# Inverting layer 3's last four half rows on ScalarE, and moving the safety flag behind the last residual

## The chip, the cores and the metric

The kernel runs on one core of one Trainium2 chip. The metric is the device time of one execution in microseconds. Three executions of the kernel before took 3706.58, 3706.09 and 3710.97 us; the median is 3706.58. One further execution was profiled. Its trace is what all rows below are from, with times counted from the start of its span.

The engines are named as in the profile: PE is TensorE's matmul, PEld its weight load, DVE is VectorE, ACT ScalarE, POOL GpSimd and SP SyncE, which here only issues DMA transfers. A `q` behind a name (SPq, DVEq) is the engine's instruction queue.

## The reference, cut to what matters

The input is four images of 56 x 56 pixels with 256 channels. Each of four layers adds to it a branch that starts with a group norm. Layer 0 is a 7x7 neighbourhood attention, layer 1 a dense graph step over chunks of 1024 tokens, layer 2 a neighbourhood attention in two dilations. The change lies in layer 3, a shifted-window attention with 8 heads of 32 channels on windows of 7 x 7 pixels:

```python
xs = jnp.roll(x, (-3, -3), axis=(1, 2))             # x: group norm of the stream
qkv = windows(xs) @ qkv_weight.T + qkv_bias         # q is scaled by 32 ** -0.5
attn = einsum('whnd,whmd->whnm', q, k) + bias + mask
attn = softmax(attn, axis=-1)
out = einsum('whnm,whmd->wnhd', attn, v) @ proj_weight.T + proj_bias
x = x + jnp.roll(windows_back(out), (3, 3), axis=(1, 2))
```

## The kernel before

`direct_blocks` does the four layers without a row maximum in its softmaxes: it takes Exp of the logits as they are, multiplies by the values, and divides by the sums. That holds only while no sum becomes too large, so all along the way sums and inverses are added into four small watch tiles. At the end `unsafe` (L2444 on) tests the sums of these tiles against a limit, and a matmul with a column of ones counts the good partitions into `flag`. Every engine reads the flag (`values_load`, L2533) and branches (L2534): where it is set, only the memset of L2535 runs; where it isn't, a second, careful implementation computes everything anew. A block with a branch hint (L2529) surrounds the test.

Layer 3 works on 32 rows of windows: row r is one of eight window rows of one of four images, with 8 windows of 49 pixels, 392 columns. A row has two halves of four heads (hq = 0, 1). Below, (30,1) is the second half of row 30. A half row goes through these steps, each of them one or two instructions per engine:

- logits (L1024): matmuls into two pairs of PSUM banks, tags `s0` and `s1`, one buffer each;
- ScalarE takes Exp of `s1` with its sum (L1028), GpSimd multiplies it with an exponentiated mask (L1029); VectorE adds the mask to `s0` (L1031), ScalarE takes its Exp (L1032);
- products (L1040): the sums over the keys, by a matmul with ones, and the products with the values, into the two banks of tag `o`, or for (30,1) and (31,1) into two buffers of tag `m`;
- finish: VectorE inverts the sums (L2295), GpSimd adds the inverse to a watch tile (L997, `seen`), and VectorE multiplies products and inverse (L2297).

The output projection of a row (`project_out`, L952) follows two rows later: matmuls into a bank, ScalarE adds the bias (L2317), GpSimd adds the residual (L2319), SyncE stores the row (L2176). Its second step also issues that store. `last_row` does row 31 by itself: it adds the bias to the residual ahead (L2333), splits the projection by the two halves of the attention (L2337), and VectorE adds straight from PSUM (L2344).

`attend_quads` runs the half rows as a pipeline: logits of one, fill work, products of the one before. In layer 3 the order on TensorE, VectorE, ScalarE and GpSimd is the order in which the code issues; SyncE's order, and all of layer 0, are left to a scheduler. After the loop the last half rows, (31,0) and (31,1), are written out by hand, with the projections of rows 29, 30 and 31 between them. The projections of row 29's second half and row 30's first half share the two banks of `s1`, and row 30's second half takes `s0`.

## Time and profile before

| what | value |
|---|---|
| median of three executions | 3706.58 us (3706.09 to 3710.97) |
| profiled execution | 3706.61 us |
| its span, first to last instruction | 3704.8 us |
| granted TensorE clock | 0.997 |
| TensorE busy, matmuls | 3646.7 us, 98% |
| VectorE, ScalarE, GpSimd busy | 59%, 40%, 49% |
| window 3680 to 3698: TensorE, VectorE, ScalarE, GpSimd busy | 13.71, 16.16, 6.63, 12.77 of 18.00 us |
| window 3698 to 3704.8: VectorE busy, all others | 0.21 us, 0 |

In a timeline row the first number is the start, the second the length from the first start to the last end of the merged instructions; then come engine, line of the kernel, operation, output and inputs, shapes and how many. In brackets stands the idle time of the engine just before and what ended it. In the chain view a row is a stretch of the path that ended last, and "issue" is time in which nothing that the profile shows was waited for.

### The profile page before, as it was taken

The numbers are of one execution on the slowest core, as the hardware profiler recorded it, in microseconds if no ns is written. First come the engines' busy times: TensorE is split into PE (matmuls) and PEld (weight loads), VectorE is DVE, ScalarE is ACT, GpSimd is POOL, SyncE is SP. The second block draws the span as 40 slices with busy tenths as digits, with TensorE's granted clock in tenths as the row PEclk, the third lists the DMA queues.
The fourth block names the chain that finished last, engine by engine and source line by source line (L and its number), as shares of the span: only waits on it lengthen the run. The fifth ranks groups of instructions, "written<-read, shape, count | busy, mean of one in ns | idle before, by whom it ended". The sixth has DMA issues, their size and how long they took to land.

```text
span 3704.8 us, 112520 instructions
## 1 busy us (share of the span) xinstructions
PE 3646.7 (98%) x48954; PEld 2480.4 (67%) x48954; DVE 2197.9 (59%) x4177; ACT 1479.3 (40%) x3137; POOL 1803.7 (49%) x1952
## 2 busy tenths in 40 slices
PE   8999999999999999999999999999999999999998
PEld 4666666677776777767777777776666666555554
DVE  5787777544445444554444643445777777677776
ACT  5666665422222222222222222223666666444444
POOL 4777877421234222352222521124877777555555
PEclk9999999999999999999999999999999999999999
DMA  7554444200011000101001000002454444544443
GB/s 232 163 168 138 145 126 135 110 7 24 24 30 38 13 19 20 29 28 23 20 19 24 27 15 11 11 21 72 120 146 144 136 131 125 166 133 134 133 134 103
DMA packets 278151, 304.95 MB, mean 82 GB/s; under 512 B 33638, under 2 KB 268778, under 8 KB 277294
## 3 DMA queue, kind: packets, MB, share of 16 engines
q1 hardware_dynamic: 275408, 296.03, 26.5%
q8 instruction: 386, 6.32, 0.7%
q10 hardware_dynamic: 672, 1.48, 0.1%
q0 software_dynamic: 1568, 0.16, 0.1%
q14 instruction: 117, 0.96, 0.1%
HBM read 205.04 MB, written 92.55 MB: 80 GB/s over the span
## 4 chain that ended last, share of the span: by engine, by line
PE 90%; DVE 5%; DMA 1%; ACT 1%; POOL 1%; issue 1%; SPq 0%; DVEq 0%; ACTq 0%; POOLq 0%
PE ps_m L952 19%; PE ps_o L1698 14%; PE ps_s L1576 14%; PE ps_v L1703 13%; PE ps_m L981 6%; PE ps_o L1113 6%; PE ps_s L1080 6%; PE ps_t L1684 3%; PE ps_o L1040 2%; PE ps_s L1024 1%; PE ps_m L1541 1%; DVE st L896 1%; DVE rs L1286 1%; DVE e L1087 1%; PE ps_m L1769 1%
## 5 line engine op out<-in xcount | busy, mean ns | idle before, releaser
L1608 DVE TENSOR_TENSOR acc<-acc,ps_v 128x257 f32<-128x257 f32 x1088 | 457.7, 422 | 774.5 <-PE ps_v L1703 751.6
L1703 PE MATMUL ps_v<-xw,e 128*128 128x257 f32 x2208 | 611.0, 381 | 3.4 <-DVE xnT L1553 2.2
L1698 PE MATMUL ps_o<-xw,at 128*128 128x257 f32 x2208 | 609.0, 379 | 0.0
L1576 PE MATMUL ps_s<-xnT,xd 128*128 128x512 f32 (+3 forms) x1344 | 571.4, 548 | 3.9 <-DVE xnT L1553 3.9
L1687 ACT COPY at<-ps_t 128x512 f32<-128x512 f32 (+3 forms) x332 | 170.7, 514 | 953.8 <-PE ps_t L1684 953.5
L1703 PEld LDWEIGHTS ps_v<-xw,e 128*128 128x128 f32 x2208 | 413.4, 189 | 144.6 <-issue 83.2
L1102 POOL TENSOR_TENSOR b<-e 124x448 f32<-124x448 f32 (+5 forms) x498 | 484.8, 995 | 7.2 <-ACT e L1088 0.3
L1698 PEld LDWEIGHTS ps_o<-xw,at 128*128 128x128 f32 x2208 | 419.1, 190 | 60.1
L952 PE MATMUL ps_m<-xn,w_wqkv 128*32 128x392 f32 x4096 | 374.3, 494 | 1.2 <-ACT xn L942 0.9
L1569 POOL TENSOR_SCALAR xd<-xnT,vec 128x128 f32<-128x128 f32 x192 | 116.3, 615 | 476.2 <-PE ps_s L1576 476.0
L1579 ACT ACTIVATE e<-ps_s 128x512 f32<-128x512 f32 x336 | 185.4, 552 | 353.0 <-PE ps_s L1576 349.7
L1576 PEld LDWEIGHTS ps_s<-xnT,xd 128*128 128x128 f32 x1344 | 225.4, 191 | 141.3 <-issue 126.2
L1091 POOL TENSOR_TENSOR e<-e,bias 119x784 f32<-119x784 f32 (+5 forms) x128 | 241.5, 1887 | 151.3 <-ACT e L1090 150.5
L1091 POOL TENSOR_TENSOR e<-e,m0t 126x672 f32<-126x672 f32 (+3 forms) x128 | 238.6, 1864 | 154.7 <-ACT e L1090 147.9
L1113 PEld LDWEIGHTS ps_o<-e,vp 124*32 124x32 f32 (+5 forms) x8000 | 193.8, 110 | 96.4 <-issue 81.5
L1002 ACT ACTIVATE no<-rs 128x168 f32<-128x168 f32 (+2 forms) x256 | 93.9, 367 | 387.7 <-DVE rs L2028 176.8
L952 PEld LDWEIGHTS ps_m<-xn,w_wqkv 128*32 128x32 f32 x4096 | 124.1, 109 | 175.7 <-issue 127.5
L2028 DVE RECIPROCAL rs<-ps_o 128x196 f32<-128x196 f32 (+2 forms) x128 | 175.7, 1373 | 101.7 <-PE ps_o L1113 82.8
L1088 ACT ACTIVATE e<-e 126x672 f32<-126x672 f32 (+5 forms) x256 | 219.6, 858 | 16.3 <-DVE e L1087 4.2
L1113 PE MATMUL ps_o<-e,vp 124*32 124x112 f32 (+5 forms) x8000 | 220.7, 248 | 0.3 <-DMA vp<-vd 0.2
L1090 ACT ACTIVATE e<-ps_s 126x672 f32<-126x672 f32 (+5 forms) x256 | 206.3, 806 | 5.4 <-PE ps_s L1080 5.4
L981 PE MATMUL ps_m<-w_wqkv,xn 128*32 128x256 f32 x3136 | 198.0, 382 | 1.8 <-DVE v L987 1.6
(240 smaller groups left out, 5985.8 us busy)
## 6 DMA issues: line engine op xcount, KB each, us to landing
x<-xr SPq DMA_DIRECT2D x64, 392.0 KB
x<-in_x SPq DMA_DIRECT2D x53, 448.0 KB
x<-x SPq DMA_DIRECT2D x60, 392.0 KB
xr<-x SPq DMA_DIRECT2D x60, 392.0 KB
vd<-v SPq DMA_DIRECT2D x72, 256.0 KB
xr<-in_x SPq DMA_DIRECT2D x32, 392.0 KB
xr<-x SPq DMA_DIRECT2D x28, 448.0 KB
x<-xr SPq DMA_DIRECT2D x28, 448.0 KB
```

Of the source, the lines that this page charges most:

```text
L952: nc.tensor.matmul(pm[j * HD:(j + 1) * HD, :n], lhsT=w[:, h, col + j * HD:col + (j + 1) * HD], rhs=rhs(h), start=(h == 0), stop=(h == CC - 1))
L981: nc.tensor.matmul(pm[i:i + HD, j * C:(j + 1) * C], lhsT=xn[:, h, first + i:first + i + HD], rhs=w[:, h, :], start=(h == 0), stop=(h == CC ...
L1080: nc.tensor.matmul(s[j // 2][:nk, j % 2, (2 * i + u) * nq:(2 * i + u + 1) * nq], lhsT=k(j, u), rhs=q(j), start=True, stop=True)
L1088: newest.append(nc.scalar.activation(ev, ev, AF.Exp))
L1090: nc.scalar.activation(ev, sv, AF.Exp)
L1091: nc.gpsimd.tensor_tensor(parts(ev), parts(ev), w["emask"], ALU.mult)
L1102: nc.gpsimd.tensor_tensor(w["b"][a][:nk, :, :2 * nq].rearrange("p h (i c) -> p h i c", i=2), ev[:, :, :, 0, :], ev[:, :, :, 1, :], ALU.add)
L1113: nc.tensor.matmul(w["o"](k, i)[j * HD:(j + 1) * HD], lhsT=ones[:nk, :HD] if k else v(j, u), rhs=w["b"][j // 2][:nk, j % 2, i * nq:(i + 1) ...
L1576: nc.tensor.matmul(s[:, :n], lhsT=xd[j][:, h, :], rhs=xnT[:, h, first * P:last * P], start=(h == 0), stop=(h == CC - 1))
L1608: nc.vector.tensor_tensor(acc[:, i, :], acc[:, i, :], pv[:, :C + 1], ALU.add)
L1698: nc.tensor.matmul(out[j][:, :C + 1], lhsT=e[:, col(i)] if i == j else at[:, col(i)], rhs=xw[:, i, :], start=(i == j), stop=(i == NB - 1))
L1703: nc.tensor.matmul(pv[:, :C + 1], lhsT=e[:, col(i)], rhs=xw[:, j, :], start=True, stop=True)
```

## The change

Six edits, all but one at the end of the kernel.

- The sums of (30,0), (30,1), (31,0) and (31,1) are no longer inverted by VectorE. ScalarE takes Ln of them and then Exp of the negative, which is the inverse; the second one also sums into a new watch tile `late` in place of GpSimd's `seen`. The Exp of L1032 of these four half rows sums into `late` too. The inversions are issued at places of their own.
- A table load for the set of activation functions that holds Exp and Ln is put at the start of `direct_blocks`; before, one was placed ahead of the first activation.
- Row 30's first half projects into `s0` and its second half into `s1`; row 31's second output tile takes `s0`.
- The watch tiles are summed earlier, apart from `late` and one other. The comparison goes to GpSimd and gives each of five columns 1/128 where it is good and less than zero where it isn't. A matmul behind the last projection adds the partitions up, and one reduction on VectorE, behind the last residual, takes the smallest of the five as the flag.
- The block with the branch hint is gone.
- The second tile of row 31's store is issued by ScalarE, the first by SyncE as before.

In the instruction order of the changed program three things shift that the diff does not name: the table load stands ahead of the loads of `vec` and `group` on ScalarE; in layer 0 two of SyncE's loads and one of VectorE's additions change places with their neighbours; at the start of layer 3 SyncE's load of the x tile of row 3 stands behind the loads of two masks, `w_wp` and `v`.

```diff
+    tables = [s.name for s in act_sets.SETS].index("natural_log_exp_and_others")
+    nc.scalar.add_instruction(mybir.InstLoadActFuncSet(..., act_func_set_id=tables, ins=[], outs=[]))
...
-            nc.scalar.activation(ev[0], ev[0], AF.Exp)
+            nc.scalar.activation(ev[0], ev[0], AF.Exp, accum_out=w.get("sum0"))
...
+            def invert():
+                rs = box["rs"] = pool.tile([P, WC], FP, tag="rs", name="rs3")
+                nc.scalar.activation(rs, box[1][:, :WC], AF.Ln)
+                nc.scalar.activation(rs, rs, AF.Exp, scale=-1.0, accum_out=late[:, i + 4:i + 5])
+
             def finish():
-                rs = pool.tile([P, WC], FP, tag="rs", name="rs3")
-                nc.vector.reciprocal(rs, box[1][:, :WC])
-                seen(rs)
+                rs = box.get("rs")
+                if rs is None:
+                    rs = pool.tile([P, WC], FP, tag="rs", name="rs3")
+                    nc.vector.reciprocal(rs, box[1][:, :WC])
+                    seen(rs)
...
-                for m, tag in enumerate(("o", "s1")):
+                for m, tag in enumerate(("o", "s0")):
...
-                    transfer(4, r, x, 1, slice(m, m + 1))
+                    transfer(4, r, x, 1, slice(m, m + 1), (nc.sync, nc.scalar)[m])
...
+        late = pool.tile([P, 8], FP, name="late", bufs=1)
+        nc.vector.memset(late, 0.0)
...
+        before[0]["invert"]()
         u3, u4 = quad(r, 0), quad(r, 1, single=True)
         out = project_out(r - 2)
         logits(u3, lambda: (out[0](), done()))
         products(held)
+        held["invert"]()
         logits(u4, held["done"])
         products(u3)
-        pair = psum_tile("s1", 1, 2)
-        out[1](pair[:, 0])
+        for i in (0, 1, 3):
+            bounds.add_up(i)
+        out[1](psum_tile("s1", 1, 2)[:, 0])
+        u3["invert"]()
+        u3["done"]()
         out = project_out(r - 1)
         first, second = last_row(r)
-        out[0](pair[:, 1])
-        u3["done"]()
+        out[0](psum_tile("s0", 1, 2)[:, 0])
         products(u4)
-        out[1](psum_tile("s0", 1, 2)[:, 0])
+        u4["invert"]()
+        out[1](psum_tile("s1", 1, 2)[:, 0])
         u4["done"]()
-        for i in (1, 3, 2):
-            add_up_watch(i)
+        bounds.add_up(4, late)
+        bounds.add_up(2)
+        bounds.compare()
         first()
         second()
+        bounds.count(ps_m(), ones[:, :1])
...
-def unsafe(tc, t, n, flag):
-    nc.vector.tensor_tensor(t[:, :n], t[:, :n], t[:, :n], ALU.mult)
-    nc.vector.tensor_scalar(t[:, :n], t[:, :n], SUM_MAX ** 2, None, ALU.is_le)
-    nc.vector.tensor_reduce(t[:, n:n + 1], t[:, :n], AX.X, ALU.min)
-        nc.tensor.matmul(ok, lhsT=t[:, n:n + 1], rhs=t[:, n + 1:], start=True, stop=True)
-        nc.vector.tensor_scalar(flag, ok, P - 0.5, None, ALU.is_ge)
+    def compare(self):
+        t = self.sums
+        self.nc.gpsimd.tensor_tensor(t, t, t, ALU.mult)
+        self.nc.gpsimd.tensor_scalar(t, t, SUM_MAX ** 2, 1.0 / P - 1.0, ALU.is_le, ALU.add)
+
+    def count(self, ps, one):
+        ok = ps[:1, :5]
+        self.nc.tensor.matmul(ok, lhsT=one, rhs=self.sums, start=True, stop=True)
+        self.nc.vector.tensor_reduce(self.flag, ok, AX.X, ALU.min)
...
-                with tc.block():
-                    tc.mark_branch_hint_location("safe", hint="LikelyTaken", engines=list(mybir.ALL_ENGINES))
-                    add_up_watch(0)
-                    unsafe(tc, bounds, n, flag)
```

## The prediction

> **What bounds the kernel now.** First the page's head, its table of busy times and its chain. TensorE is busy 98% of the span, and the chain that ended last is 90% TensorE.
>
> ```profile
> span 3704.8 us, 112520 instructions
> PE 3646.7 (98%) x48954; PEld 2480.4 (67%) x48954; DVE 2197.9 (59%) x4177; ACT 1479.3 (40%) x3137; POOL 1803.7 (49%) x1952
> PE 90%; DVE 5%; DMA 1%; ACT 1%; POOL 1%; issue 1%; SPq 0%; DVEq 0%; ACTq 0%; POOLq 0%
> ```
>
> So an edit that does not take matmuls away can only gain where TensorE is not the one that ends last. The edits lie in the last 27 us. There I read the timeline of each engine from 3678.7 us on. VectorE first:
>
> ```profile
> 3678.93 2.61 DVE L2295 RECIPROCAL rs<-ps_o 128x392 f32<-128x392 f32 x1 [1.75 <-PE ps_o L1040]
> ...
> 3682.96 2.60 DVE L2295 RECIPROCAL rs<-ps_m 128x392 f32<-128x392 f32 x1
> ...
> 3686.15 0.97 DVE L1031 TENSOR_TENSOR e<-ps_s,m3b 98x784 f32<-98x784 f32 x1
> 3687.03 2.60 DVE L2295 RECIPROCAL rs<-ps_o 128x392 f32<-128x392 f32 x1
> ...
> 3690.88 2.61 DVE L2295 RECIPROCAL rs<-ps_m 128x392 f32<-128x392 f32 x1 [0.64 <-PE ps_m L1040]
> ...
> 3695.89 0.69 DVE L2344 TENSOR_TENSOR xr<-xr,ps_s 128x343 f32<-128x343 f32 x3
> 3696.49 0.56 DVE L2526 TENSOR_REDUCE bounds<-watch 128x1 f32<-128x392 f32 x1
> ...
> 3698.01 0.15 DVE L2453 TENSOR_SCALAR flag<-n_safe 1x1 int32<-1x1 f32 x1 [0.37 <-PE n_safe L2452]
> 3703.13 0.06 DVE L2535 MEMSET flag<- 1x1 int32 x1 [4.97 <-issue]
> ```
>
> VectorE works almost without a gap: four reciprocals of 2.6 us, and behind the last residual (3696.58) another 1.58 us of bound checks up to the flag (3698.16). Then TensorE and ScalarE, which wait meanwhile:
>
> ```profile
> 3685.37 1.50 PE L952 MATMUL ps_s<-attn,w_wp 128*32 128x392 f32 x16
> 3688.54 1.52 PE L952 MATMUL ps_s<-attn,w_wp 128*32 128x392 f32 x16 [1.67 <-ACT pr L2317]
> ```
> ```profile
> 3684.92 0.19 ACT L1028 ACTIVATION_READ_ACCUMULATOR e<-ps_s 98x1 f32 x1
> 3687.16 0.86 ACT L1032 ACTIVATE e<-e 98x784 f32<-98x784 f32 x1 [2.04 <-DVE e L1031]
> 3687.92 0.57 ACT L2317 ACTIVATE pr<-ps_s,vec 128x392 f32<-128x392 f32 x1
> ```
>
> TensorE stands idle 1.67 us because L2317 of the projection sits on ScalarE behind the Exp of L1032, which waits for L1031 on VectorE, which stands behind a reciprocal. Last, the chain at the very end: after the flag has been read, 3.93 us in which nothing runs but the branch.
>
> ```profile
> 3698.20 0.54 DVEq L2533
> ...
> 3698.90 3.93 issue
> ```
>
> **Reciprocals to ScalarE.** Removed: 4 x 2.6 us of L2295 on VectorE and 4 x 1.03 us of L997 on GpSimd. Added: on ScalarE four Ln and four Exp of 128x392, each taken as 0.57 us (L2317, same shape, from PSUM), and eight accumulator reads of 0.19 (L1028). No row shows an Ln. Lower bound 0.52 (0.86 of L1032 less half its elements at about 0.33), upper bound 0.86 (a whole L1032); I take 0.57, the same shape. A pair with its read is 0.57 + 0.05 + 0.57 + 0.11 = 1.3 us, against 2.65 for the reciprocal.
>
> I follow the new order, engine by engine, with a half row as (row, half). (30,0): its sums are ready at 3678.8; Ln and Exp take ScalarE to 3680.2, so L2297 ends at 3680.8 (before 3682.15), and L1031 of (31,0) at 3681.8 (before 3683.04). The L1028 behind the pair slips from 3679.83 to 3680.2. Its next waiter, L1029, has 1.8 us of idle time before it. L1032 of (31,0), now with an accumulator, runs 3681.87 to 3682.8. Ln and Exp of (30,1) follow to 3684.1; L2297 to 3684.7, L1031 of (31,1) to 3685.7 (before 3687.12). What is queued behind this pair is L1028 of (31,1), whose logits TensorE has by 3683.65: it starts at 3684.12, as early as before (3684.20), because the pair stands where the wait stood.
>
> TensorE then takes L952 of row 29 when that L1028 frees the bank, 3685.10 (before 3685.37). Row 30's first half goes to the other bank (the tags are swapped), free at 3685.7, so it starts 1.32 us later, at 3686.42, in place of 3688.54. From there TensorE never waits in my sum: products of (31,1) from 3687.76 (1.34 later; L1029 is done at 3687.0), row 30's second half 3689.14 (1.38), first halves of row 31 at 3690.46 and 3691.12 (1.32, 0.66), the second half at 3691.78 (0.66). Before it was 3694.22: 2.44 us won. ScalarE must keep up: L1032 of (31,1) to 3686.7, L2317 to 3687.3, pair to 3688.5, L2317 to 3689.1, pair to 3690.4, L2317 (waits for TensorE) to 3691.3, two L2333 to 3692.4. L2297 of (31,1) ends at 3691.0, 0.75 us before TensorE wants it. L2344 comes 0.99 us after the second half's start, as before: 3692.77, with the second tile to 3694.14.
>
> **Flag.** The check over 392 columns, L2447 and L2448 leave the end: the sums move ahead, where VectorE now waits, and two small operations go to GpSimd behind its last L2319 (3692.7) and end at 3693.2 (0.20 and 0.22 each by L925 and L926). The count on TensorE stands behind its last matmul and waits for GpSimd: 3693.5. Left behind the residual is one reduction of 0.16 (L2449): flag at 3694.33, before 3698.16. That is 3.83 us, all of it on the end's chain. If GpSimd were late, its cover is the 0.6 us from 3693.5 to the residual's end.
>
> **Two queues.** On SyncE the last two transfers' issue (0.81 us) goes to ScalarE. SyncE's first pair ends at 3694.4 and delays its flag read by 0.07. ScalarE issues from 3694.2 to 3695.05 and branches 0.8 us after the others; SyncE meets it only at the closing barrier, whose waits take SyncE over 1 us after the branch: nothing. The writes themselves run under the 3.9 us of the branch, as before.
>
> **Branch.** The block with a prefetch hint and its two jumps go. In the DMA view no instruction transfer lies between 3692.6 and 3698.0, where the hints stand, and the instruction queues run only from 3699.7 on, after the branch. So the hint fetched nothing; I take 0. Bounds: 0.5 us less, if the fetch no longer follows so close behind the output's writes, and another fetch round, 3.9 us more.
>
> **Table load.** It moves ahead of two DMA issues on ScalarE. The trace shows one load of 1.28 us, and `vec` landing at 3.83 (L853 starts on it). `vec` lands up to 1.28 us later, at 5.1. VectorE uses it now between the two first statistics (4.58 to 5.13), and the next tile lands at 5.97: covered. SyncE's seventh load waits for the first tile (4.53) instead of `vec` (3.93), with six tiles of 1.2 us ahead of it: covered. Layer 0's other shifted loads are used microseconds later. I take +0.1, bounds -0.5 and +1. The changed program has one table load on this path, and the trace no switch to price. The Trainium skill (ScalarE: Activation LUTs, section What ACT_TABLE_LOAD costs) states an estimated price for what speaks against this edit: 2.66 us for each switch of the set of functions. By it, eight switches between Ln and Exp would add 21 us, and the sum would be 3724. The same page lists one set that holds both, the one loaded here, and by that the sum stays.
>
> **Layer 3's opening.** A 0.06 us memset shifts SyncE's order: the x load (392 KB) goes behind two mask loads, w_wp and v. TensorE waits 0.6 us for v at 3220.15 (list of waits); v comes about 1 us sooner. The x tile then lands near 3220, its 1.66 us of L945 end just before VectorE's next job (3222.02). Gain between 0 and 0.6; I take 0.3.
>
> **Sum.** 3.76 + 0.3 - 0.1 = 4.0 us. The profiled execution took 3706.61 (span 3704.8 and 1.8 around it), beside a median of 3706.58. Forecast 3702.6 us. A measurement of this kernel tells about 0.2% (7.4 us) from no change; this is 0.11%.
>
> **Rivals.** (a) The branch costs one more fetch round without its hint: 3702.6 + 3.85 = 3706.4. For it: 3.93 us even with the hint, so the code is not at hand. Against it: no transfer by the hint. (b) Slower: the sequencers, unhinted, run on into the fallback's code and fetch two rounds before the target's. Place: after the flag read; price 7.7 us; 3710.3. It decides from 4.0 us on. (c) ScalarE becomes the bound: Ln and Exp cost 0.86 each. The pairs of (30,0) and (30,1) lie on the path to 3685.10 and add 1.2 us; the last two add 1.2, less the 0.75 of slack: 0.4. Then 3702.6 + 1.6 = 3704.2. For it: my ScalarE row is full from 3686.7 to 3690.4. (d) More is won: layer 0 and layer 3's opening give their 0.5 and 0.6, and the fetch is quicker by 3 us beside idle queues: 3699 or less. Nothing in the profile speaks for the last. (e) The new flag reads false and the fallback runs: thousands of us more; the five sums of 128 times 1/128 are exact, so 1%.
>
> **How the numbers follow.** Forecast 0.60, (a) 0.13, (b) 0.07, (c) 0.13, (d) 0.06, (e) 0.01. The forecast's own bounds: layer 0's -0.6 and +0.9, layer 3's opening -0.3 and +0.3, the branch -0.5, a shorter Ln and Exp -0.2, the two close runs' 0.5 either way: 3700.5 to 3704.3. Range 3700.5 to 3707.0: above it takes in (a) with the same 0.5. Forecast, (a) and (c) hold 0.86, some 0.8 with runs like the third (3710.97). Faster by over 0.2% (below 3699.2): (d) and a little of the spread, 0.08. Slower (above 3714.0): half of (b), and (e), 0.04. Within: 0.88.
>
> **What would show it.** No reciprocal of L2295's kind after the one at 3673.98; TensorE without a gap over 0.3 us from the second-half projection of row 29 to the end; flag about 0.2 us after the last residual; some 3.9 us from flag read to the closing memset. A gap on TensorE that ends on ScalarE's Ln or Exp shows (c); 7 us or more after the flag shows (a) or (b). Wrong would be a shift before 3670 us of more than 1 us.

## The result, and the profile after

| | median | runs | lowest to highest |
|---|---|---|---|
| before | 3708.55 us | 22 | 3705.74 to 3713.31 |
| after | 3702.86 us | 22 | 3699.03 to 3707.31 |

The ratio is 0.9987, with a 95% interval of 0.9981 to 0.9993: 4.8 us less by the ratio, 5.7 us by the two medians, 2.6 to 7.0 us by the interval. That is inside the 0.2% which the prediction called no measurable change, though over 22 runs of each kernel the interval lies clear of 1, and the time is 0.3 us from the forecast of 3702.6. Some of that is luck: the forecast stood on a before of 3706.6, and over 22 runs before is 2 us slower than that. What is to be tested is the forecast's gain, 4.0 us, and where it came from.

The head of the page of after. All but 1% of TensorE's time is still busy; VectorE has lost 11 us of work, ScalarE gained 3.

```profile
span 3703.0 us, 112515 instructions
PE 3647.8 (99%) x48954; PEld 2482.7 (67%) x48954; DVE 2186.7 (59%) x4171; ACT 1481.9 (40%) x3153; POOL 1799.1 (49%) x1950
```

The span of this profile is only 1.8 us shorter than before's 3704.8. So the two were laid over each other, matmul by matmul, and the shift was read at a few places (after minus before, at before's time):

| before's time | shift | what lies between |
|---|---|---|
| 620 | +0.12 us | layer 0 |
| 704 | +4.3 | the change from layer 0 to layer 1 |
| 3149.8 | +4.4 | layers 1 and 2 |
| 3166.7 | +3.0 | end of layer 2 |
| 3207.9 | +2.9 | |
| 3220.2 | +1.65 | opening of layer 3 |
| 3677.2 | +1.63 | layer 3, up to the products of half row (30,0) |
| end | -1.8 | the edited tail |

The edited tail won 3.43 us (3.44 in the table below, which counts from the tail's own start) and the opening of layer 3 won 1.2. The other steps, +4.2 and -1.4, lie where no instruction was changed. First the tail. VectorE's timeline in after: the last reciprocal is that of 3675.61, from then on VectorE has waits of 0.9 to 2.9 us, and the flag stands 0.06 us behind the last residual.

```profile
3675.61 2.60 DVE L2307 RECIPROCAL rs<-ps_o 128x392 f32<-128x392 f32 x1
...
3681.74 0.57 DVE L2309 SCALAR_TENSOR_TENSOR attn<-ps_o,rs 128x392 f32<-128x392 f32 x1 [2.93 <-ACT rs L2301]
...
3686.77 0.94 DVE L2481 TENSOR_REDUCE bounds<-watch 128x1 f32<-128x392 f32 x3
...
3694.30 0.69 DVE L2357 TENSOR_TENSOR xr<-xr,ps_o 128x343 f32<-128x343 f32 x3 [1.99 <-POOL xr L2332]
3694.91 0.68 DVE L2357 TENSOR_TENSOR xr<-xr,ps_s 128x343 f32<-128x343 f32 x3
3695.51 0.14 DVE L2493 TENSOR_REDUCE flag<-ps_m 1x1 int32<-1x5 f32 x1
3701.08 0.06 DVE L2562 MEMSET flag<- 1x1 int32 x1 [5.43 <-issue]
```

ScalarE does one of the inversions, and TensorE's rows of the same stretch:

```profile
3680.56 0.50 ACT L2300 ACTIVATE rs<-ps_o 128x392 f32<-128x392 f32 x1 [1.17 <-PE ps_o L1043]
3681.09 0.53 ACT L2301 ACTIVATE rs<-rs 128x392 f32<-128x392 f32 x1
3681.52 0.19 ACT L2301 ACTIVATION_READ_ACCUMULATOR rs<-rs 128x1 f32 x1
3681.62 0.80 ACT L1031 ACTIVATE e<-ps_s 98x784 f32<-98x784 f32 x1
```
```profile
3686.61 2.82 PE L955 MATMUL ps_s<-attn,w_wp 128*32 128x392 f32 x32
3689.25 0.86 PE L1043 MATMUL ps_m<-e,ones 98*32 98x98 f32 x32
3689.93 0.86 PE L1043 MATMUL ps_m<-e,v 98*32 98x98 f32 x32
3690.61 1.50 PE L955 MATMUL ps_s<-attn,w_wp 128*32 128x392 f32 x16
3691.93 0.84 PE L2350 MATMUL ps_o<-attn,w_wp 128*32 128x392 f32 x8
```

Row 29's second-half projection and row 30's first half are one group of 32 matmuls without a gap, where before stood a wait of 1.67 us; TensorE's rows have no bracket with idle time from there to the count. Then the chain of after at the very end, where before had a flag read of 0.54 and 3.93 us of "issue":

```profile
3695.69 0.83 DVEq L2560
3696.52 0.08 issue
3696.60 0.07 DVEq L2561
3696.67 4.10 issue
```

The flag comes 4.14 us earlier than before, counted from the products of (30,0), but from the flag to the end it takes 7.34 us, not 6.64.

Second, the shift of +4.2 us between 620 and 704 us. The windows view of that stretch, of before and then of after (columns: window, its length, busy time of five engines, granted clock, DMA share, GB/s):

```profile
620.00:704.00 84.00, 77.20 (x1142) 54.32 (x1136) 56.64 (x86) 41.82 (x74) 56.21 (x52) 0.94 0.31 95
```
```profile
620.00:704.00 84.00, 76.71 (x1126) 54.21 (x1120) 55.25 (x81) 40.52 (x72) 53.71 (x48) 0.90 0.26 82
```

The granted clock was lower in after's execution. The trace's record of the clock has it at half speed for 10.24 us in this stretch of before and for 17.07 us in that of after, in pieces of 3.41 us. Whether this comes with the change or by chance is one question for the experiments.

### The profile page after: what moved, and what is told of

It reads as the page before. It is cut to its first block, busy times and chain, and to the rows that moved or that the text cites. A ratio compares the mean times of both kernels' runs of the same rounds, so it can differ in the third digit from the quotient of the medians.

```text
span 3703.0 us, 112515 instructions
## 1 busy us (share of the span) xinstructions
PE 3647.8 (99%) x48954; PEld 2482.7 (67%) x48954; DVE 2186.7 (59%) x4171; ACT 1481.9 (40%) x3153; POOL 1799.1 (49%) x1950
## 4 chain that ended last, share of the span: by engine, by line
PE 90%; DVE 5%; POOL 1%; DMA 1%; ACT 1%; issue 1%; SPq 0%; DVEq 0%; ACTq 0%; POOLq 0%
PE ps_m L955 19%; PE ps_o L1701 14%; PE ps_s L1579 14%; PE ps_v L1706 13%; PE ps_m L984 6%; PE ps_o L1116 6%; PE ps_s L1083 5%; PE ps_t L1687 3%; PE ps_o L1043 2%; PE ps_s L1027 2%; PE ps_m L1544 1%; POOL b L1105 1%; DVE e L1090 1%; DVE rs L1289 1%; DVE st L899 1%
```

## The experiments

The theory: the gain is made at two places, the tail (inversions off VectorE, other banks, flag behind the residual) and the opening of layer 3 (SyncE's order); everything else in which the two profiles differ is chance. The rivals: the other shifts belong to the change; one part of the change does all the work, or none; the end pays for something that the prediction costed at nothing.

All 14 profiles were read in the same way. "To residual" runs from the start of the products of (30,0) to the end of the last residual, "SyncE branch" is the time from the flag to SyncE's branch, "wait" that from its branch to its next instruction, "opening" runs from the logits at 3207.87 to the v products at 3220.15 (times of before). "Half speed" is TensorE's half-speed time ahead of the products of (30,0) (behind them and before the flag only no_table has any, one piece of 3.41), and "rest" the span up to those products without the opening. All in us:

| kernel | to residual | to flag | SyncE branch | wait | flag to end | tail | opening | half speed | rest |
|---|---|---|---|---|---|---|---|---|---|
| before | 19.34 | 1.58 | 0.59 | 3.82 | 6.64 | 27.56 | 12.28 | 13.65 | 3665.0 |
| before_again | 19.33 | 1.58 | 0.58 | 3.79 | 6.60 | 27.51 | 11.93 | 10.24 | 3663.8 |
| no_hint_block | 19.33 | 1.58 | 0.59 | 3.20 | 6.02 | 26.94 | 12.08 | 17.07 | 3668.9 |
| no_hint_block_again | 19.33 | 1.58 | 0.59 | 3.53 | 6.35 | 27.26 | 11.95 | 6.83 | 3661.0 |
| no_hint | 21.01 | 0.59 | 1.31 | 3.64 | 7.18 | 28.77 | 12.28 | 10.24 | 3666.0 |
| after | 16.72 | 0.06 | 0.97 | 4.14 | 7.34 | 24.12 | 11.05 | 17.07 | 3667.8 |
| after_again | 16.72 | 0.06 | 0.98 | 4.02 | 7.23 | 24.01 | 11.24 | 17.07 | 3670.6 |
| late_pool | 16.72 | 0.06 | 0.99 | 4.02 | 7.24 | 24.02 | 12.26 | 10.24 | 3662.8 |
| no_invert | 20.51 | 0.06 | 0.78 | 3.95 | 6.96 | 27.53 | 11.53 | 6.83 | 3665.3 |
| no_table | 27.03 | 0.06 | 1.17 | 3.77 | 7.17 | 34.25 | 11.05 | 10.24 | 3667.0 |
| old_banks | 17.70 | 0.06 | 0.99 | 3.66 | 6.87 | 24.63 | 11.23 | 13.65 | 3667.7 |
| act_queue | 16.72 | 0.06 | 0.86 | 3.55 | 6.64 | 23.42 | 11.19 | 20.48 | 3670.4 |
| split_store | 16.72 | 0.06 | 0.83 | 4.13 | 7.19 | 23.97 | 11.05 | 20.48 | 3670.1 |
| combo | 16.78 | -0.60 | 0.65 | 3.38 | 6.45 | 22.63 | 11.05 | 10.24 | 3664.6 |

Three programs are in it twice. Their "to residual" and "to flag" repeat to 0.01 us, SyncE's wait to 0.03 to 0.33, the opening to 0.13 to 0.35.

### The same programs again

No edit. First the kernel before:

> The kernel before, unchanged: what two sets of runs of one program differ by, and a second profile of it. Theory CHANCE: the shift of +4.2 us between TensorE's 620 and 704 us that the profile of after has against that of before goes with TensorE's half-speed stretches (17.07 us before the last matmul against 13.65) and has nothing to do with the change; so in this second profile of the same program these stretches again differ by one or more pieces of 3.41 us, and the span moves by 1.0 to 1.7 us for each piece; the end of layer 2 (16.86 us from TensorE's event at 3149.80 to that at 3166.66 in before, 15.45 in after) also comes out different by over 0.5 us though the program is the same. Theory CODE: both belong to the program: half-speed 13.65 us again and 16.86 us again, each within 0.2. The opening of layer 3 (from the logits at 3207.87 to the v products at 3220.15: 12.28 us) and the tail (from the sums' products of half row (30,0) to the end: 27.56 us = 19.34 to the last residual's end + 1.58 to the flag + 6.64 to the end) should repeat within 0.2 us under both. The times should be 3708 to 3709 in the median, ratio 1.000 with an interval of some +-0.0006.

Measured: median 3708.38 us beside 3707.49 for before, ratio 1.0003 (0.9993 to 1.0012). One piece of half speed less and "rest" 1.2 us less; the end of layer 2 took 17.37 us in place of 16.86. CHANCE holds on both, at the end of layer 2 only just (0.51 us where it asked for over 0.5): the same program moves between executions at the very places where after had moved against before. The tail repeats to 0.05 us; the opening only to 0.35.

And the kernel after:

> The kernel after, unchanged: a second profile, and a second measurement of the whole change. Theory: the parts that belong to the program repeat (16.7 us from the products of (30,0) to the last residual, 0.06 to the flag, opening of layer 3 11.0 to 11.6 us), those that do not belong to it move (half-speed stretches before the last matmul by whole pieces of 3.41 us; the end of layer 2; SyncE's wait behind the branch, 3.55 to 4.14 us so far). In all profiles so far the end came 2.23 us after SyncE's first instruction behind the branch, whatever the other engines did: the same here within 0.02. Ratio to before between 0.9980 and 0.9992: of 4.6 us, 3.4 to 3.9 at the tail and 0.4 to 1.2 at layer 3's opening, 0.9988.

Measured: 3704.18 us, ratio 0.9987 (0.9978 to 0.9996): the gain, 4.8 us by the ratio, is there a second time. To the residual 16.72 again, flag 0.06, end 2.23 us behind SyncE's first instruction. Its end of layer 2 took 18.01 us, against 15.45 in the first profile: the 1.4 us that after seemed to win there was not the change's.

Over the 14 profiles "rest" rises by 0.55 us for each us of half speed (a straight line through the 14 points, correlation 0.86), near the half that is to be expected of it: a piece of 3.41 us costs 1.7 to 1.9 us. After's first profile has one piece more than before's; without it its span would have been about 3.6 us below before's, not 1.8. The Trainium skill ("TensorE: Matmul & The Clock Gate", Part 1) tells of a free-running window of 3413 ns, and has TensorE's clock go to half after at least one such window of idleness. The pieces here are 3.413 us long or whole multiples of it, which agrees. But the clock dropped here in a stretch in which TensorE was busy for 77 of 84 us, with no wait over 1.3 us in its rows: in this case no idle window of that length came ahead of the drop, and the measurement decides.

### Inversions back on VectorE

```
-            of_late = {} if r < NIMG * 8 - 2 else dict(sum0=late[:98, i:i + 1], invert=invert)
+            of_late = {} if r < NIMG * 8 - 2 else dict(sum0=late[:98, i:i + 1], invert=no_step)
```

> The kernel after with the last four inversions back on VectorE (2.6 us each) and their bound sums on GpSimd; banks, flag and queues stay as in after (the bound on the last two half rows' sums is added up too early and so is not tested: that part of the check is left out). Theory INVERSION (the prediction's): VectorE is again the one that ends last; the reciprocals of (31,0) and (31,1) then follow each other without the bank wait, from 3688.1 to 3693.9 in before's time, L2309 ends at 3694.6, and the last residual ends 19.5 to 19.9 us after the products of (30,0) start (after: 16.72; before: 19.34), the flag 0.1 later, 26.9 to 27.4 in all to the end (after: 24.12), so about 3 us slower than after. Rival BANKS: the bank swap alone had freed TensorE, and the inversions were hidden: 16.7 to 17.5 us to the last residual, under 1 us slower than after.

Measured: 3706.08 us, ratio 0.9995 (0.9985 to 1.0005). To the residual 20.51, in all 27.53: 3.4 us more than after. VectorE's timeline:

```profile
3687.61 0.95 DVE L2481 TENSOR_REDUCE bounds<-watch 128x1 f32<-128x392 f32 x3 [0.95 <-POOL watch L1000]
3688.48 2.60 DVE L2307 RECIPROCAL rs<-ps_o 128x392 f32<-128x392 f32 x1
...
3691.60 2.60 DVE L2307 RECIPROCAL rs<-ps_m 128x392 f32<-128x392 f32 x1
3694.31 0.57 DVE L2309 SCALAR_TENSOR_TENSOR attn<-ps_m,rs 128x392 f32<-128x392 f32 x1
```

INVERSION holds: the two last reciprocals, one behind the other, set the end, though TensorE has its other banks. The 0.6 to 1.0 us over the expected 19.5 to 19.9 are the bracket of the first row: the bound's sum stands on VectorE ahead of the reciprocals and waits there 0.95 us for GpSimd's addition. The experiment made that wait; less it, the residual would end near 19.6 (an estimate: 20.51 less 0.95), still 2.8 us later than in after.

### Banks as before

```
-            for m, tag in enumerate(("o", "s0")):
+            for m, tag in enumerate(("o", "s1")):
...
-        out[1](psum_tile("s1", 1, 2)[:, 0])
+        pair = psum_tile("s1", 1, 2)
+        out[1](pair[:, 0])
...
-        out[0](psum_tile("s0", 1, 2)[:, 0])
+        out[0](pair[:, 1])
...
-        out[1](psum_tile("s1", 1, 2)[:, 0])
+        out[1](psum_tile("s0", 1, 2)[:, 0])
```

> The kernel after with the banks of the last projections as in before: the second half of row 29 and the first half of row 30 share the pair of bank tag s1, the second half of row 30 has s0, the last row's second tile has s1. Theory BANK (the prediction's): the first half of row 30 must again wait until ScalarE's L2330 has read the second half of row 29, which it does from 3688.24 to 3688.83 in the profile of after; TensorE then starts it at 3688.9 in place of about 3687.9, a gap of 0.9 us, and as TensorE had no gap to give back behind it, the last residual ends 17.5 to 17.8 us after the products of (30,0) start (16.72 in after), the total to the end is 24.9 to 25.2 (24.12). Rival FREE: with the inversions gone from VectorE the pair is read in time, or TensorE's order has slack: 16.7 to 16.9. The median is 0.8 us at most above after's, less than the times can tell.

Measured: 3703.42 us, ratio 0.9987 (0.9977 to 0.9996); to the residual 17.70, 0.98 more than in after. TensorE's timeline:

```profile
3686.66 1.50 PE L955 MATMUL ps_s<-attn,w_wp 128*32 128x392 f32 x16
3688.93 1.52 PE L955 MATMUL ps_s<-attn,w_wp 128*32 128x392 f32 x16 [0.77 <-ACT pr L2330]
```

BANK holds: row 30's first half waits for ScalarE's reading of row 29, and nothing behind it gives the time back. So of the 2.62 us by which the last residual came earlier, 1.0 needs the banks as well as the inversions.

### No explicit table load

```
-    tables = [s.name for s in act_sets.SETS].index("natural_log_exp_and_others")
-    nc.scalar.add_instruction(mybir.InstLoadActFuncSet(name=nc.get_next_instruction_name(), act_func_set_id=tables,
-                                                       ins=[], outs=[]))
```

> The kernel after without the explicit load of the table set at its start. The program then has 17 table loads in place of 9 (both branches counted): eight more, one ahead of each Ln and one ahead of each Exp that follows another function, all in the last 25 us. Theory PRICE: each costs ScalarE what the one in the trace takes (1.28 us), about 10 us in all, and ScalarE becomes the engine that ends last: each pair takes 1.3 + 2.6 us, the last residual ends 5 to 10 us later than in after (21.7 to 26.7 us after the products of (30,0) start, 16.72 in after), the median 3708 to 3713. By the skill's page (2.66 us for a switch) it would be 21 us: 3724. Rival HIDDEN: ScalarE has gaps of 0.4 to 1.2 us between its pieces in after, the loads run in them and the end moves by under 2 us. At the start: the load goes back behind the two DMA issues; layer 0's first 20 us should move by under 0.2 us under both.

Measured: 3715.38 us, ratio 1.0020 (1.0011 to 1.0030); to the residual 27.03 us, 10.31 more than after. ScalarE's timeline, one inversion:

```profile
3679.72 1.28 ACT L2297 ACT_TABLE_LOAD   x1 [1.16 <-PE ps_o L1040]
3681.01 0.50 ACT L2297 ACTIVATE rs<-ps_o 128x392 f32<-128x392 f32 x1
3681.53 1.28 ACT L2298 ACT_TABLE_LOAD   x1
3682.82 0.53 ACT L2298 ACTIVATE rs<-rs 128x392 f32<-128x392 f32 x1
```

PRICE holds: each of the eight loads takes the 1.28 us, and the last residual comes 10.31 us later, 0.3 beyond the expected 5 to 10. That eight loads make 10.24 us is in part a coincidence. In this profile TensorE waited 2.48 us for ScalarE and then ran 32 matmuls in 4.52 us that take 2.82 in after, at a granted clock of 0.62 over those 4.52 us, and ScalarE waited for them in its turn:

```profile
3690.52 4.52 PE L952 MATMUL ps_s<-attn,w_wp 128*32 128x392 f32 x32 [2.48 <-ACT e L1028]
3693.49 0.59 ACT L2327 ACTIVATE pr<-ps_s,vec 128x392 f32<-128x392 f32 x1 [1.34 <-PE ps_s L952]
```

From there to the last Exp ScalarE has no gap. At full clock the 1.34 us would hardly be there, so the loads by themselves are worth some 9.0 us of the 10.31 (an estimate: the difference of the two); the rest of their 10.24 would then lie in gaps that ScalarE has in after. Whether the loads, by making TensorE wait, also brought the half clock about was not tried. The explicit load, 3680 us ahead of its use, makes the inversions on ScalarE a gain: without it the tail is 6.7 us longer than before's. The Trainium skill's 2.66 us for a switch ("ScalarE: Activation LUTs", section What ACT_TABLE_LOAD costs) is 1.28 us of load and 1.38 of drain; here no drain shows: the load stands 0.02 us behind the Ln, and the Exp 0.01 behind the load. The measurement decides: 1.28. HIDDEN falls. This execution was also 1.5 us late at 20 us already, because one x tile of layer 0 landed some 1.3 us late; with the explicit load that place is reached anywhere from 19.96 to 21.01 us, so it can't be said that the missing load did it.

### The opening of layer 3

```
-        nc.vector.memset(late, 0.0)
+        nc.gpsimd.memset(late, 0.0)
```

> The kernel after with one instruction moved: the zeroing of the tile `late` (128x8) is done by GpSimd in place of VectorE. That alone puts SyncE's order at the opening of layer 3 back as it is in before: the x load of a later row goes ahead of the loads of m3c, m3b, w_wp and v. Theory ORDER: the opening's 1.2 us gain (from the logits at 3207.87/3210.75 to the v products at 3220.15/3221.80: 12.28 us in before, 11.05 in after) comes from that order, so it is 12.1 to 12.4 here, with TensorE's wait for v of 0.6 us back. Rival CHANCE: the loads merely landed sooner in that execution: 11.0 to 11.3 here. The tail stays at 24.1 us under both. The median should be 0 to 1.3 us above after's, within what the times can tell.

Measured: 3702.98 us, ratio 0.9990 (0.9981 to 1.0000); opening 12.26. TensorE's timeline at v, in before, in after, in this kernel, and in before's second profile:

```profile
3218.21 1.31 PE L1040 MATMUL ps_o<-e,ones 98*32 98x98 f32 x32
3220.15 0.89 PE L1040 MATMUL ps_o<-e,v 98*32 98x98 f32 x32 [0.63 <-DMA v<-vd]
```
```profile
3221.10 0.89 PE L1043 MATMUL ps_o<-e,ones 98*32 98x98 f32 x32
3221.80 0.86 PE L1043 MATMUL ps_o<-e,v 98*32 98x98 f32 x32
```
```profile
3216.05 1.09 PE L1043 MATMUL ps_o<-e,ones 98*32 98x98 f32 x32
3217.96 0.89 PE L1043 MATMUL ps_o<-e,v 98*32 98x98 f32 x32 [0.82 <-DMA v<-vd]
```
```profile
3217.05 0.89 PE L1040 MATMUL ps_o<-e,ones 98*32 98x98 f32 x32
3218.63 0.89 PE L1040 MATMUL ps_o<-e,v 98*32 98x98 f32 x32 [0.70 <-DMA v<-vd]
```

ORDER holds. The six profiles in which SyncE issues the x load first have an opening of 11.93 to 12.28 us (mean 12.13), the eight with v first one of 11.05 to 11.53 (mean 11.17): 1.0 us. The bracket shows only a part of what the wait for v costs. With the x load first, v's products start 0.63 to 0.85 us behind the end of the products with the ones; with v first they start about 0.2 us before that end, as two groups do that follow each other without a wait (3221.80 against 3221.10 + 0.89 in after). In before the products with the ones are stretched as well, to 1.31 us, but the gain does not rest on that: in three of the six profiles with the x load first, before's second one among them, they take 0.89 us and the opening is still 11.93 to 12.08. Why they are stretched in some profiles was not tried.

### The hint of the branch

```
                 with tc.block():
-                    tc.mark_branch_hint_location("safe", hint="LikelyTaken", engines=list(mybir.ALL_ENGINES))
                     add_up_watch(0)
                     unsafe(tc, bounds, n, flag)
```

This is the second of two kernels, profiled twice; the first took the block away as well. The branch's label, to which the hint refers, goes in both.

> The kernel before with the hint of the branch and its block removed, nothing else (the check's instructions stand where they stood). Theory NOTHING (the prediction's): the hint fetched nothing, so the branch costs the same: 3.6 to 4.1 us from the branch to each engine's next instruction, 6.5 to 6.7 us from the flag to the end, 27.4 to 27.6 us from the products of (30,0) to the end (27.56 and 27.51 in the two profiles of before). Rival FETCH (the prediction's rivals a and b): without it one or two more rounds of 3.9 us: 10.5 or 14.4 us from the flag to the end, and the median 3711 or 3715. Rival GAIN: up to 0.5 us less, because the two jumps of the block go.

> The kernel before with the hint's instruction alone removed: the block around the check, its two jumps and the order of every other instruction stay. (Where the block went too, VectorE's sum over the 392 columns moved ahead of the last residual and waited 1.10 us for GpSimd; so that run could be read for the branch alone.) Theory NOTHING: 20.9 us from the products of (30,0) to the flag (20.92 and 20.91 in the two profiles of before), 6.3 to 6.9 from the flag to the end, 27.2 to 27.8 in all. Rival FETCH: one more round of 3.9 us behind the branch: over 10 us from the flag to the end.

> The kernel before without the hint's instruction, a second profile. In the first, SyncE waited 3.20 us behind its branch, where the two profiles of before have 3.82 and 3.79, and the flag-to-end time was 6.02 in place of 6.64 and 6.60. Theory HINT: the hint costs SyncE that 0.6 us, and its removal gives it back: 3.1 to 3.3 us again, 5.9 to 6.2 to the end. Theory CHANCE: the wait moves from execution to execution within what all kernels showed (3.20 to 4.14): a value over 3.4 here; 6.2 to 7.0 to the end.

Measured: without hint and block 3709.04 us, ratio 1.0001 (0.9991 to 1.0010); without the hint alone 3709.66 and 3702.10 us in one run each, 17.07 and 6.83 us of them at half speed. The waits behind the branch are 3.64, 3.20 and 3.53 us on SyncE and 3.57 to 4.17 on the other engines, as in the other kernels: FETCH falls, rivals (a) and (b) with it. What the first expectation said of the order was wrong: the block had kept the sum of 392 columns behind the residual. Without it VectorE meets the sum first:

```profile
3696.90 0.56 DVE L2526 TENSOR_REDUCE bounds<-watch 128x1 f32<-128x392 f32 x1 [1.10 <-POOL watch L997]
```

and the residual comes 1.7 us later. Of the 0.6 us by which the second kernel's flag-to-end was shorter, the repeat shows half to be CHANCE (3.53 where the first had 3.20). Whether the hint costs the other 0.3 us stays open: SyncE's wait lies between 3.20 and 4.14 us over all profiles, and kernels without the hint have both the shortest and the longest.

### What the end pays for

Two kernels that change only what goes on around the flag's read.

```
-                    transfer(4, r, x, 1, slice(m, m + 1), (nc.sync, nc.scalar)[m])
+                    transfer(4, r, x, 1, slice(m, m + 1), nc.scalar)
```

> The kernel after with both of the last row's stores issued by ScalarE, none by SyncE. In after SyncE reads the flag 0.31 us after it is written, because it is still issuing the first tile's store, and the end comes 7.34 us after the flag (6.64 in before, 6.60 in its second profile). Theory ISSUE: that late read is what the end pays for: SyncE then reads at +0.03, branches at 0.65 to 0.95 and the end comes 0.3 to 0.4 us sooner: 6.9 to 7.05 after the flag. Theory TRAFFIC: the read of the flag itself is what got longer (0.83 us on VectorE at 366 GB/s of DMA traffic, 0.54 at 190 GB/s in before), on every engine alike; taking the issue away from SyncE leaves the read at 0.8, and SyncE's branch moves only from +0.97 to about +0.92: 7.2 to 7.35. Rival SCALAR: ScalarE, which issues all four transfers and reads the flag at about +1.2, becomes the last: over 7.4. The last residual stays at 16.7 us under all.

```
-                if m:
+                if r == NIMG * 8 - 2:
+                    transfer(4, r, x, 1, slice(m, m + 1))
+                elif m:
                     transfer(4, r, x, 1)
```

> The kernel after with row 30's store (392 KB, issued in one piece when GpSimd has finished both halves) issued in two pieces, each when its half is ready; nothing else moves. Theory TRAFFIC: the flag's read takes 0.83 us in after because that store runs under it (366 GB/s, all DMA engines busy); with half of the store gone 2.5 us earlier the read takes 0.5 to 0.65 us on VectorE, TensorE and GpSimd, and the end comes 0.15 to 0.35 us sooner: 7.0 to 7.2 us after the flag in place of 7.34 (7.24 in the kernel with `late` zeroed by GpSimd). Theory ISSUE: the read is long for another reason (SyncE's and ScalarE's DMA issues at the same time): it stays at 0.8, and the end at 7.2 to 7.4. The last residual stays at 16.7.

Measured: act_queue 3703.31 us, ratio 0.9985 (0.9976 to 0.9995), flag to end 6.64; split_store 3702.46 us, ratio 0.9982 (0.9973 to 0.9992), flag to end 7.19. From the chain of split_store, VectorE's read of the flag:

```profile
3697.98 0.55 DVEq L2562
```

and the windows view of VectorE's flag read, in after and then in split_store:

```profile
3695.69:3696.52 0.83, 0.00 (x0) 0.00 (x0) 0.00 (x0) 0.00 (x0) 0.00 (x0) 1.00 1.03 361
```
```profile
3697.98:3698.53 0.55, 0.00 (x0) 0.00 (x0) 0.00 (x0) 0.00 (x0) 0.00 (x0) 1.00 0.59 202
```

TRAFFIC holds for the read: with half of row 30's store gone sooner it takes 0.55 us in place of 0.83, and 0.55 to 0.56 in place of 0.78 to 0.79 on TensorE and GpSimd. What in the traffic does it stays open: in after the reads of SyncE and ScalarE, which begin 0.27 and 0.90 us later than VectorE's, take 0.59 and 0.58 us with the DMA engines as busy. The end moves by less, since SyncE's wait behind the branch came out long (4.13). For act_queue the result was better than any of the three theories had it, and the table says why: SyncE's branch moved by 0.11 us, not far from what TRAFFIC had (0.05), since its read, begun at once, now took 0.76 us; and its wait was short (3.55). The columns share one rule: the end stands 2.23 us behind SyncE's first instruction after the branch, in 13 of the 14 profiles to 0.01 us (branch 0.97 + wait 4.14 + 2.23 = 7.34 in after; 0.59 + 3.82 + 2.23 = 6.64 in before). SyncE's closing list of waits is what ends last. VectorE's memset, on which the chain view ends, is met inside that list.

### A version with all of it

Both edits above; the two comparisons of the bounds on VectorE, the count on TensorE and the minimum on VectorE between the last row's two tiles:

```
-        self.nc.gpsimd.tensor_tensor(t, t, t, ALU.mult)
-        self.nc.gpsimd.tensor_scalar(t, t, SUM_MAX ** 2, 1.0 / P - 1.0, ALU.is_le, ALU.add)
+        self.nc.vector.tensor_tensor(t, t, t, ALU.mult)
+        self.nc.vector.tensor_scalar(t, t, SUM_MAX ** 2, 1.0 / P - 1.0, ALU.is_le, ALU.add)
...
                 half(m, 1)
+                if m == 0:
+                    bounds.count(ps_m(), ones[:, :1])
                 for w, xv in parts(pms[m], x[:, m, :]):
                     newest[:] = [nc.vector.tensor_tensor(xv, xv, w, ALU.add)]
+                if m == 0:
+                    bounds.decide()
```

> The kernel after with three things that shorten SyncE's way from the flag to the branch: row 30's store in two pieces, both of the last row's stores issued by ScalarE, and the flag decided earlier (the two comparisons on VectorE, which is idle then, the count on TensorE between the two tiles of the last second half, and the minimum on VectorE between the two tiles' residuals). Theory SYNC: the end is SyncE's first instruction behind the branch + 2.23 us. SyncE then reads the flag at once, in 0.5 us, some 16.3 us after the products of (30,0) start and not at 17.1, and branches at 16.9 (17.75 in after): 22.7 to 23.3 us from the products of (30,0) to the end (24.12 in after, 24.0 to 24.6 in its variants); the last residual 0.15 later than in after (16.87), because the minimum stands before its second tile. Rival SCALAR: ScalarE, which then issues four transfers before it reads the flag, is the last: it goes on at 21.9 to 22.3, SyncE's closing list waits for it at its end, and the end is 22.9 to 23.4 all the same, but later than SyncE's first instruction + 2.23. Rival READ: the engines' reads of the flag are not the limit, 24 us again. The median should be 0.8 to 1.4 us below after's, less than the times can tell; ratio to before 0.9978 to 0.9990.

Measured: 3703.44 us, ratio 0.9985 (0.9976 to 0.9994); in the same comparison after has 3704.18 and 0.9987. VectorE's timeline:

```profile
3691.10 0.69 DVE L2361 TENSOR_TENSOR xr<-xr,ps_o 128x343 f32<-128x343 f32 x3 [1.58 <-POOL xr L2332]
3691.71 0.14 DVE L2502 TENSOR_REDUCE flag<-ps_m 1x1 int32<-1x5 f32 x1
3691.78 0.67 DVE L2361 TENSOR_TENSOR xr<-xr,ps_s 128x343 f32<-128x343 f32 x3
```

SYNC holds. The tail is 22.63 us, 1.4 to 1.5 below after's: 0.9 from SyncE's earlier branch (16.83 us behind the products of (30,0), 17.75 in after), 0.6 to 0.8 from a short wait (3.38) that may be chance, and 0.2 lost again because SyncE's list has to wait for the landing of the last store, which ScalarE issued, a small share of SCALAR. The direction is shown by the profile; the times of the two kernels cannot be told apart.

## Why the prediction was right, and where its sizes were off

Its sum was 3.76 (tail) + 0.3 (opening) - 0.1 (layer 0) = 4.0 us. The runs give 3.43 and 3.50 (the first and the second pair of profiles) + 1.0, with layer 0 lost in the noise: 4.5 us, a ratio of 0.9988 where 0.9987 was measured twice. The 1.2 us between these 4.5 and the two medians' 5.7 lie within the interval, so the runs do not show that there is more to explain. That 4.0 came so near to 4.5 is luck in part, because misses cancel: 0.3 us more up to the flag, 0.6 to 0.7 less behind it, 0.7 more at the opening.

- **Reciprocals to ScalarE: right, 0.2 us too small.** The Ln took 0.48 to 0.50 us and the Exp 0.53, not 0.57 each; a pair with its read keeps ScalarE 1.06 us, not 1.3. The last residual came 2.62 us earlier, not 2.44. TensorE's predicted start of row 29's second half, put on after's time base (+1.63), is 3686.73, measured 3686.61; the last second half 3693.41, measured 3693.24. Rival (c), with 0.86 for each, falls.
- **Banks: right.** The step "row 30's first half goes to the other bank" is worth 1.0 us, shown by undoing it.
- **Flag: right.** It comes 4.14 us earlier in place of 3.83. Of these 0.31 us 0.18 are the residual's, counted above; the other 0.13 are the step's own: the flag stands 0.06 us behind the residual, not 0.19.
- **Two queues and branch: the step that failed.** It had 0.07 us for SyncE and nothing for ScalarE. From the flag to the end it takes 0.63 to 0.70 us more. SyncE reads the flag 0.28 us late, because the first tile's store is still being issued: the prediction let that issue end 0.07 behind the flag, but the flag came 0.3 us sooner than it thought. The read itself is 0.1 us longer on SyncE, as on ScalarE, and 0.3 on the three other engines under row 30's store, which the prediction didn't look at. The remaining 0.2 to 0.3 us are the wait behind the branch (4.14 and 4.02 against 3.82 and 3.79); it varies by up to 0.3 us between executions of one program, and whether a part of it belongs to the change stays open. What it said of ScalarE held: its branch, 0.6 us behind the others, costs nothing. What it missed is that SyncE's own branch, with the list of waits behind it, is what sets the end, so that each tenth that SyncE is late counts in full.
- **Hint: right.** No fetch is added by its removal; that it gives back 0.3 us is open.
- **Table load: right in size, not in its reason.** Layer 0 lost 0.07 us at 20 us and 0.12 at 620. VectorE's use of `vec` moved between the two first statistics as said, but the load did not make `vec` late: ScalarE issued it at 0.76 us, 0.03 later than in before, while the load ran. The price of leaving the load out, for which the trace had no row, is 10.3 us in one profile, some 9.0 of them the loads' own.

```profile
0.72 1.28 ACT L842 ACT_TABLE_LOAD   x1 [0.72 <-PEq L2550]
0.76 0.43 ACTq L853 DMA_DIRECT2D vec<-in_vec  x1
```

- **Opening of layer 3: right in kind, 0.7 us too small.** The mechanism is the one named, v ahead of the x load, but it gave 1.0 us against 0.3, beyond the bound of 0.6. The prediction counted the wait in the bracket alone and took the middle between nothing and its 0.6 us; but without the wait v's products also begin 0.2 us before the group in front of them ends, the wait itself is up to 0.85 us in other profiles, and in after's profile none of the gain is lost again: the shift is +1.65 at 3220 and +1.63 at 3677.
- **What would make it wrong.** "A shift before 3670 us of more than 1 us" did occur (+1.63, and +4.4 on the way) and did not make the prediction wrong. The criterion was: it took one execution for the program. Its sign for rivals (a) and (b), 7 us or more after the flag, occurred as well (7.34 and 7.23) without either rival: each had priced a fetch round at over 3.8 us, and the 0.6 to 0.7 us here are SyncE's late read, its longer read and its wait. The sign lay only 0.4 above before's 6.64. A bound of 0.5 us for executions of the same code, from two close runs, is too small; "rest" spans 9.5 us over the 14 profiles.

## What to carry to other kernels

Where a change is worth a thousandth, lay the two traces over each other and take the gain from the edited stretches alone: there they repeat to 0.35 us, while the untouched rest moved by up to 9.5 us with the granted clock and with the landing of transfers. An inversion as exp(-ln) on an idle ScalarE pays where VectorE's reciprocal stands on the path, if one table set with both functions is loaded early, and if the banks let TensorE use what it wins. At the end of a program ask which engine's closing list is last, and keep DMA issues and full DMA queues away from that engine's read of a flag.

## What the runs showed that was not expected

- An engine's read of one flag takes 0.5 us, but 0.8 us where a store of 392 KB was issued 1.5 us ahead of it and the DMA engines are full. Busy DMA engines alone don't do it: in the last kernel the read takes 0.55 us with them 90% busy, and in after the read that begins 0.27 us later takes 0.59.
- Behind a taken branch every engine waits 2.9 to 4.2 us for its next instruction, and not always the same one is first; the program's end follows SyncE's first instruction by 2.23 us.
- TensorE's clock drops to half for whole pieces of 3.41 us where the program passes from one layer to the next (around 630 to 680 and 3165 us), two to six such pieces in an execution, five and two in two executions of one program, and each costs 1.7 us by the clock and 1.9 by the line through the 14 profiles. That goes a long way to explain the spread of some 8 us between runs of one kernel. Only in no_table does a piece fall between the products of (30,0) and the flag.
- A switch of ScalarE's table set costs 1.28 us, and no drain is to be seen. ScalarE issues a transfer while a table load runs (0.76 us in a load from 0.72 to 2.00).
